# Layer 3's first sums and LayerNorms moved beside the last expert tiles of layer 2, in a four-layer conv/attention kernel

## The chip, the cores and the metric

The kernel runs on one core of a Trainium2 chip. Its time is that of the device, in microseconds; a kernel is timed several times and the median is given. Besides that, one execution is taken by the hardware profiler: from it come the busy times, waits and start times below. Times inside the profile count from the start of its span.

## The reference, cut to what matters

The input is four images of 256 channels by 32 x 32, so 4 x 1024 tokens of 256 numbers, float32. Layers 0 and 1 (a convolutional state-space block and a non-local block) come first and the change does not touch them. Layers 2 and 3 work on tokens:

```python
t = t + _L2_attn_ref(_ln_t(t), ...)     # softmax attention within an image
t = t + _L2_ffn_ref(_ln_t(t), ...)      # 8 experts, each token goes to its best 2
t = t + _L3_attn_ref(_ln_t(t), ...)     # "lambda" attention, see below
t = t + _L3_ffn_ref(_ln_t(t), ...)      # an LSTM over the 1024 tokens of each image
```

with, for the experts and for layer 3's attention,

```python
for e in range(E):
    h = gelu(xf @ W1[e] + b1[e])
    out = out + w_dense[:, e:e + 1] * (h @ W2[e] + b2[e])
...
sm = softmax(key, axis=1)                        # over the tokens of an image
lam = einsum('bnd,bne->bde', sm, value)          # 256 x 256 for each image
bn = (lam - mean) * rsqrt(var + BN_EPS)          # over images and columns
return einsum('bnd,bde->bne', query, bn * gamma + beta)
```

So each image's `lam` needs all its tokens after the experts, and the batch norm over `lam` needs all four images. The LSTM starts behind that and is a chain of 1024 steps.

## The kernel before, in words

**Experts (layer 2).** Each image's tokens are sorted by expert as soon as its attention and routing are done: POOL scatters them to a DRAM array `sorted`. The experts then run over tiles of 256 sorted places (`TS`), or 128 in a "half" tile. The 36 tiles (`NTILE`) are 17 "first" ones (`NFULL`), which hold only tokens known before the last image was routed; 16 "more" (`NMORE`); and 3 halves (`NHALF`). A half follows after every five or six of the "more" tiles. The last image's routing (`_head`, `_other_tiles`) runs as a generator in steps beside the first tiles. Up to three more halves stand behind a branch (`tc.If(need > NHALF)`), which this input does not take.

For each tile POOL fetches the expert's weights (2.2 MB, three buffers, two tiles ahead) and the rows by indirect DMA. PE transposes the rows (`pt`) and DVE copies them out (`uT`, L1279). PE makes 8 blocks of hidden units (`ph`, L1300), to which ACT applies the GELU (L1292), and two outputs (`po`, L1334), which DVE scales (`y`, L1339 and L1340). POOL scatters `y` to the DRAM array `results` (L1341), which has two places for each token, one for each of its two experts. In a half tile `ph` (L1314) has the tokens as its rows, DVE copies it out (`raw`, L1318) and PE transposes it back (L1322).

**Layer 3's attention** (`_layer3_attention`) starts behind the branch. For each image SP loads the two sums of four blocks (`y_in`, L1486, 0.5 MB each), DVE adds them to the tokens `s.xr` (L1491) and takes the statistics (L1495, L1496); a reciprocal root is made by 13 small DVE operations, ACT writes the normalised `rows` (L1476), and PE turns them to channels (`p_x`, L1442), from where DVE copies them to `u` (L1446). PE then makes the keys (`p_mm`, L1517), ACT moves them out (L1522), DVE takes the maximum (`top`, L1529), ACT the exponential (L1532). PE turns the keys back in eight pieces (`p_k`, L1542), which DVE copies (`kt`, L1544), and multiplies them with the rows (`p_u`, L1546); two more products give `lam` (L1556, L1560). PE also turns `s.xr` itself (L1442) and ACT copies it to a second array of channels (`x_l3`, L1445). The first image is put ahead by hand (`_in_order`, and `later` for what follows).

Behind the four images come the queries (L1573), the batch norm of `lam` (L1592), and the LSTM with its first products (`beside`, from L1674). The LSTM's constants (`_lstm_constants`: `fold`, `mask`, `shift`, `b_l`) and weights (`w_l`, `w_u`, `w_v`) are made and loaded right behind the branch. The LSTM's outputs are kept where `s.x` was.

**What sets the order.** Each engine works through its own queue in order. The tile framework's scheduler orders the instructions of a function by priorities and dependences, and inserts the waits; where the code says `_in_order`, the order as written stands. A tile pool that is opened where another was closed takes its memory, and its first users wait for the last ones of the old. Transfers on POOL's, SP's and ACT's queues share 16 DMA engines.

## Time and profile before

| what | us |
|---|---|
| median of 3 runs (3392.86 to 3399.31) | 3398.27 |
| the profiled execution | 3408.06 |
| its span | 3406.3 |
| PE, DVE, ACT, POOL busy | 3177.1, 1997.0, 1233.9, 378.8 |
| first tile's `ph` begins | 783.8 |
| one full tile, one half tile | 14.25, 8.3 |
| last expert matmul ends | 1306.7 |
| first product of layer 3 (`p_x`) | 1324.7 |
| `lam` of images 0, 1, 2, 3 (L1556) begins | 1363.8, 1394.1, 1418.5, 1442.2 |
| first LSTM step, first with a hidden state | 1472.1, 1475.3 |
| one LSTM step | 1.9 |

A profile line names the engine, the line of the code, the operation, and the tiles written and read, with a count. In a timeline the first number is the start and the second the length; a bracket at the end gives the idle time before it and what ended it. In a table by stretches, each pair is the busy time of an engine and its number of instructions; then come the clock granted to PE as a part of the full one, the share of the DMA engines and GB/s.

### The profile page before, as it was taken

Reading aid. Unit: us, or ns where it says so; the run is one execution under the profiler, and the core shown is the slowest. Engines: PE = TensorE matmul, PEld = TensorE weight load, DVE = VectorE, ACT = ScalarE, POOL = GpSimd, SP = SyncE. Lnnn points to the kernel's source line nnn. Section 1 sums busy time; section 2 is a strip of 40 time slices with the busy share of each in tenths; the row PEclk is TensorE's granted clock in tenths of the full one; section 3 lists DMA queues with packets and bytes.
Section 4 is the critical chain, followed back from the end, with each engine's and each line's share of the span. In section 5 each row is a group of like instructions: output and inputs, shape, how many; then the busy total and the mean of one; then the engine's idle time right before and its main releaser. Section 6 shows DMA issues by size and latency. Waiting matters only on the chain.

```text
span 3406.3 us, 146430 instructions
## 1 busy us (share of the span) xinstructions
PE 3177.1 (93%) x65186; PEld 2489.1 (73%) x65186; DVE 1997.0 (59%) x8389; ACT 1233.9 (36%) x5057; POOL 378.8 (11%) x468
## 2 busy tenths in 40 slices
PE   7788899998899996999999999999999999999888
PEld 4465344446788884688888888888888888888776
DVE  5696534452211115557777777776777767776666
ACT  4633222223222222433434334343343343443333
POOL 0083002223433330000000000000000000000000
PEclk9899899999999997999999999999999999999999
DMA  1291001115555654000000000000000000000000
GB/s 69 67 298 34 10 0 38 38 36 203 187 195 206 230 212 148 0 3 5 4 11 4 5 11 4 11 4 4 11 4 5 10 4 5 10 5 4 10 4 10
DMA packets 78058, 180.50 MB, mean 53 GB/s; under 512 B 6256, under 2 KB 63920, under 8 KB 72816
## 3 DMA queue, kind: packets, MB, share of 16 engines
q0 software_dynamic: 14880, 106.99, 8.5%
q1 hardware_dynamic: 60624, 59.12, 5.9%
q8 instruction: 511, 8.37, 1.0%
q10 hardware_dynamic: 1920, 5.00, 0.4%
q14 instruction: 123, 1.01, 0.1%
HBM read 111.26 MB, written 59.84 MB: 50 GB/s over the span
## 4 chain that ended last, share of the span: by engine, by line
PE 72%; DVE 14%; ACT 5%; issue 3%; DMA 2%; POOL 1%; ACTq 0%; DVEq 0%; POOLq 0%
PE p_c L1826 11%; PE p_c L1817 8%; PE ph L1300 6%; PE po L1334 6%; DVE turned L1867 6%; PE p_i L1817 5%; PE p_o L1826 5%; PE p_i L1826 5%; PE p_o L1817 5%; PE beside L1767 4%; PE p_mm L850 3%; PE p_s L814 2%; ACT a_o L1868 2%; DVE x L1880 2%; ACT th L1878 1%
## 5 line engine op out<-in xcount | busy, mean ns | idle before, releaser
L1868 ACT ACTIVATE add<-turned 128x8 f32<-128x8 f32 x1024 | 214.3, 209 | 1011.4 <-DVE turned L1867 1011.4
L1826 PE MATMUL p_c<-w_v,x 128*4 128x64 f32 x16368 | 416.7, 219 | 60.6 <-DVE x L1880 57.9
L1817 PE MATMUL p_c<-xg,shift 128*128 128x64 f32 x2048 | 446.0, 299 | 0.0
L1826 PE MATMUL p_o<-w_v,x 128*4 128x64 f32 x16368 | 417.8, 219 | 0.0
L1826 PE MATMUL p_i<-w_v,x 128*4 128x64 f32 x16368 | 417.4, 219 | 0.0
L1817 PE MATMUL p_i<-xg,shift 128*128 128x64 f32 x2048 | 407.7, 281 | 0.0
L1867 DVE STREAM_TRANSPOSE turned<-p_c 128x64 f32<-128x64 f32 x1024 | 255.7, 250 | 253.9 <-PE p_c L1826 220.0
L1817 PE MATMUL p_o<-xg,shift 128*128 128x64 f32 x2048 | 396.4, 275 | 0.0
L1817 PEld LDWEIGHTS p_c<-xg,shift 128*128 128x128 f32 x2048 | 304.9, 188 | 117.6 <-DVE turned L1867 0.4
L1826 PEld LDWEIGHTS p_c<-w_v,x 128*4 128x4 f32 x16368 | 227.9, 85 | 180.8 <-DVE x L1880 102.0
L1880 DVE TENSOR_TENSOR x<-a_o,th 128x8 f32<-128x8 f32 x1024 | 171.2, 167 | 246.0 <-ACT th L1878 246.0
L1817 PEld LDWEIGHTS p_o<-xg,shift 128*128 128x128 f32 x2048 | 311.4, 192 | 0.0
L1817 PEld LDWEIGHTS p_i<-xg,shift 128*128 128x128 f32 x2048 | 305.1, 188 | 0.0
L1826 PEld LDWEIGHTS p_o<-w_v,x 128*4 128x4 f32 x16368 | 281.9, 87 | 0.8 <-issue 0.5
L1826 PEld LDWEIGHTS p_i<-w_v,x 128*4 128x4 f32 x16368 | 281.6, 87 | 0.3
L1867 DVE STREAM_TRANSPOSE turned<-p_i 128x64 f32<-128x64 f32 x1024 | 271.9, 266 | 0.9 <-PE p_i L1826 0.7
L1292 ACT ACTIVATE hT<-ph,w 128x256 f32<-128x256 f32 (+1 forms) x288 | 131.3, 465 | 355.8 <-PE ph L1300 267.3
L1300 PE MATMUL ph<-uT,w 128*128 128x256 f32 x1056 | 241.6, 386 | 19.6 <-DVE uT L1279 11.3
L1867 DVE STREAM_TRANSPOSE turned<-p_o 128x64 f32<-128x64 f32 x1024 | 255.6, 250 | 0.9 <-PE p_o L1826 0.3
L1334 PE MATMUL po<-w,hT 128*128 128x256 f32 x1104 | 251.1, 380 | 2.7 <-ACT hT L1292 1.5
L1868 ACT ACTIVATE a_o<-turned 128x8 f32<-128x8 f32 x1024 | 213.3, 208 | 95.4 <-DVE cell L1871 4.5
L1300 PEld LDWEIGHTS ph<-uT,w 128*128 128x128 f32 x1056 | 203.2, 194 | 50.2 <-DVE uT L1279 12.1
(499 smaller groups left out, 4395.0 us busy)
## 6 DMA issues: line engine op xcount, KB each, us to landing
sorted<-zeros SPq DMA_DIRECT2D x32, 1032.0 KB
y_in<-results SPq DMA_DIRECT2D x16, 512.0 KB
x<-in_x_dram SPq DMA_DIRECT2D x8, 512.0 KB
tokens<-rows SPq DMA_DIRECT2D x4, 1024.0 KB
x<-tokens SPq DMA_DIRECT2D x8, 512.0 KB
out_dram<-x_l SPq DMA_DIRECT2D x64, 64.0 KB
results<-y,place POOLq DMA_INDIRECT x69
w_l<-in_w_l_dram ACTq DMA_DIRECT2D x1, 1092.0 KB
```

The source lines that it names most:

```text
L814: nc.tensor.matmul(p_s[:, h, :], q[:, k, q0 : q0 + P], u[:, k, b * L + h * W : b * L + (h + 1) * W], start=k == 0, stop=k == C - 1,)
L850: nc.tensor.matmul(p, v[:, n, bass.ts(c, P)], prT[:, n, :], start=n == 0, stop=n == TPI - 1,)
L1292: nc.scalar.activation(hT[:, n, : A * P], ph, AF.Gelu, bias=b1[:, n : n + 1])
L1300: nc.tensor.matmul(ph, w1[:, k, bass.ts(n, P)], uT[:, k, :], start=k == 0, stop=k == C - 1,)
L1334: nc.tensor.matmul(po, hT[:, n, bass.ts(a, P)], w2[:, n, :], start=n == 0, stop=n == NHC - 1,)
L1767: nc.tensor.matmul(p[bass.ts(i, R), :], rows[:, k, bass.ts(g, R)], w_u[:, k, at : at + GQ // GC], start=k == 0, stop=k == C - 1, tile_posi ...
L1817: nc.tensor.matmul(p[:, :H], shift[:, row * B : row * B + P], xg[n][:, g, bass.ts(i, H)], start=True, stop=t == 0,)
L1826: nc.tensor.matmul(p[R * i : R * i + B, :H], hs[:, t - 1, bass.ts(k, B)], w_v[:, k, i * GQ + g * H : i * GQ + (g + 1) * H], start=False, s ...
L1867: nc.vector.transpose(zt.rearrange("p c w -> p (c w)"), pz[g][:, :H])
L1868: nc.scalar.activation(dst.rearrange("p (c b) -> p c b", c=C), zt[:, :, :B], f)
L1878: nc.scalar.activation(th, cell[:, :, 1], AF.Tanh)
L1880: nc.vector.tensor_mul(h, a_o, th)
```

## The change

It does five things.

1. *The order of the tiles.* The "more" tiles are 14 that may hold tokens of any image, and then, interleaved with the three halves, two that hold only the last image's tokens or are empty. `NLAST` (31) is the number of tiles that may hold tokens of the first three images. `_other_tiles` places them by four kinds instead of two.
2. *Two sets of pools.* The experts are split into `_first_experts` (17 tiles) and `_last_experts` (the rest), with pools opened anew between them, since layer 3's buffers now share the memory with the second part. `hT` has one buffer and `uT` two.
3. *Image 0 and 1 beside the last tiles.* `_rows_to_u` holds the loads, sums, statistics, rows and transposes of an image as a generator. Those of image 0 run in steps beside tiles 32 and 33, those of image 1 beside tiles 34 and 35. The loads are declared independent of the scatters of tiles 31 to 35. They have two buffers of 0.5 MB. The instructions of these tiles stand in the order as written.
4. *Behind the branch:* keys of image 0 together with the rows of image 2, rows of image 3 with keys of image 1, then keys of images 2 and 3 with the transposes of x. The `p_k`/`p_u` loop issues the next transpose ahead of the last product. The keys have one buffer.
5. *x in place.* The channel copy of x is written over the tokens it came from (`s.x3`), and the LSTM's outputs get an array of their own. Weights of the LSTM and its constants are loaded or made after the attention.

```diff
+NLAST = (2 * (T - L) + E * (TS - 1)) // TS
...
+        m.order = [("first", i) for i in range(NFULL)]
+        m.order += [("more", i) for i in range(NLAST - NFULL)]
+        for i in range(NHALF):
+            m.order.append(("half", i))
+            if NLAST - NFULL + i < NMORE:
+                m.order.append(("more", NLAST - NFULL + i))
...
+            _layer2_attention(s, m)
+            _first_experts(s, m)
+        _last_experts(s, m)
...
+def _last_experts(s, m):
+    nc, tc = s.nc, s.tc
+    m.late, m.early = [], []
+    with ExitStack() as ctx:
+        wp = ctx.enter_context(tc.tile_pool(name="l3_w", bufs=1))
+        l3 = SimpleNamespace(
+            pool=ctx.enter_context(tc.tile_pool(name="l3", bufs=2)),
+            row=ctx.enter_context(tc.tile_pool(name="l3_row", bufs=2)),
+            y=ctx.enter_context(tc.tile_pool(name="l3_y", bufs=2)),
+            ps=ctx.enter_context(tc.tile_pool(name="l3_ps", bufs=2, space=PSUM)),
+            banks=0,
+            w=wp.tile([P, C, 2 * D], F32, name="w_kv"),
+        )
+        nc.scalar.dma_start(
+            l3.w, s.d["w_l3"][:, D : 3 * D].rearrange("(k p) n -> p k n", p=P)
+        )
...
+        parts = [_rows_to_u(s, l3, b) for b in range(2)]
...
+            fetched(NFULL + 1)
+            ahead = [_turned(s, m, NFULL)]
+            for j in range(NFULL, NTILE):
+                if j + 2 < NTILE:
+                    fetched(j + 2)
...
+                def beside(n):
+                    if j > NLAST:
+                        for _ in range(2 if m.order[j][0] == "half" else 1):
+                            next(parts[(j - NLAST - 1) // 2], None)
+                if j == NLAST:
+                    next(parts[0])
+                done = _worked(s, m, j, *ahead.pop(), lead, beside)
+                if j >= NLAST:
+                    _in_order(s, start)
...
+            for got in m.early:
+                for put in m.late:
+                    for one, other in ((got, put), (put, got)):
+                        tc.declare_no_dep(
+                            one.ins, other.ins, reason="these tiles hold the last image's tokens"
+                        )
...
+def _rows_to_u(s, l3, b, split=False):
...
+    def load():
+        g, k = todo[len(ys)]
+        at = k * T + (b * G + g) * W
+        y = l3.y.tile([P, TPB, D], F32, name="y_in")
+        got = nc.sync.dma_start(
+            y, s.results[at : at + W, :].rearrange("(j p) c -> p j c", p=P)
+        )
+        if b < B - 1:
+            l3.early.append(got)
+        ys.append(y)
...
+    load()
+    load()
+    yield
+    for i, (g, k) in enumerate(todo):
+        xr = s.xr[:, bass.ts(b * G + g, TPB), :]
+        nc.vector.tensor_add(xr, xr, ys[i])
+        if len(ys) < len(todo):
+            load()
+        yield
+        if k == 1:
+            for j in range(TPB):
+                stats = l3.pool.tile([P, nc.vector.BN_STATS_DIM], F32, name="stats")
+                nc.vector.bn_stats(stats, xr[:, j, :])
+                nc.vector.bn_aggr(mv[:, g * TPB + j, :], stats)
+                if j % 2:
+                    yield
...
+def _layer3_last_image(s, l3):
...
+        wq = wp.tile([P, C, D], F32, name="wq")
+        nc.scalar.dma_start(wq, s.d["w_l3"][:, 3 * D :].rearrange("(k p) n -> p k n", p=P))
...
+        order = (
+            (_keys(s, l3, 0, nc.vector), _rows_to_u(s, l3, 2)),
+            (_rows_to_u(s, l3, 3, split=True), _keys(s, l3, 1, nc.scalar)),
+            (_keys(s, l3, 2, nc.vector), chain(by_channel(0), by_channel(1))),
+            (_keys(s, l3, 3, nc.vector), chain(by_channel(2), by_channel(3))),
+        )
+        for parts in order:
+            for _ in _in_turn(*parts):
+                pass
+        for _ in queries():
+            pass
...
-        hs = s.x.rearrange("p c b l -> p (c b l)").rearrange("p (l s) -> p l s", s=S)
+        bias, fold, mask, shift = _lstm_constants(s, keep)
+        w_u = _weights(s, keep, "w_u")
+        w_v = _weights(s, keep, "w_v")
+        wq = keep.tile([P, C, D], F32, name="wq")
+        nc.scalar.dma_start(wq, s.d["w_l3"][:, :D].rearrange("(k p) n -> p k n", p=P))
+
+        hs = keep.tile([P, L, S], F32, name="hs")
```

Lines of the changed kernel that the prediction names: the adds are L1593, `shift` L1565, `rows` L1571, the transposes of the rows L1579, the y loads L1553, the first `ph` L1331.

## The prediction

> **What bounds the kernel now.** I read in this order: the page (who is busy), the chain that ended last, PE's timeline from the last expert tiles to the first LSTM step, and the other engines' timelines across the same stretch. The page says PE is busy 93% of the span and the chain that ended last lies 72% on PE, so what counts is where PE stands still and how long its stages last. PE around the branch:
>
> ```profile
> 1294.76 3.62 PE L1334 MATMUL po<-w,hT 128*128 128x256 f32 x16
> 1298.21 3.60 PE L1314 MATMUL ph<-w,uT 128*128 128x512 f32 x8
> ...
> 1303.08 3.62 PE L1334 MATMUL po<-w,hT 128*128 128x256 f32 x16
> 1324.72 2.16 PE L1442 MATMUL p_x<-ident,rows 128*128 128x128 f32 x8 [18.02 <-ACT rows L1476]
> 1328.64 3.63 PE L1517 MATMUL p_mm<-u_l,w_l 128*128 128x512 f32 x4 [1.76 <-DVE u_l L1446]
> ```
>
> Experts end at 1306.7 (call it E), and PE then stands 18.0 us. The other engines say what fills it: the last scatter, the load of its sums, two adds, LayerNorm.
>
> ```profile
> 1311.73 1.19 DVE L1411 TENSOR_REDUCE fold<-ident 128x32 f32<-128x128 f32 x4 [4.18 <-DMA w<-in_w_dram,half_rows]
> ...
> 1316.41 1.23 DVE L1491 TENSOR_TENSOR x<-x,y_in 128x1024 f32<-128x1024 f32 x1 [3.15 <-DMA y_in<-results]
> 1317.90 1.23 DVE L1491 TENSOR_TENSOR x<-x,y_in 128x1024 f32<-128x1024 f32 x1 [0.26 <-DMA y_in<-results]
> ```
>
> Both DVE and ACT go on 5.0 us after E (scatter issued by POOL at 1307.83, then 3.9 us to what waits for it); the first load, issued 1311.91, is added 4.5 us later. The stretches from E to the queries:
>
> ```profile
> 1306.70:1324.70 18.00, 0.00 (x1) 0.00 (x0) 9.72 (x34) 0.63 (x2) 0.97 (x1) 0.63 0.68 238
> 1324.70:1363.80 39.10, 30.57 (x97) 17.52 (x97) 29.66 (x86) 11.85 (x20) 0.00 (x0) 0.73 0.56 180
> 1363.80:1394.20 30.40, 26.64 (x117) 17.90 (x118) 23.11 (x79) 15.08 (x29) 0.00 (x0) 0.94 0.00 1
> 1394.20:1418.60 24.40, 23.49 (x113) 16.31 (x113) 12.22 (x24) 10.93 (x20) 0.00 (x0) 1.00 0.00 1
> 1418.60:1442.20 23.60, 20.59 (x87) 13.33 (x86) 7.35 (x16) 8.42 (x14) 0.00 (x0) 1.00 0.00 0
> ```
>
> Length, then busy time of PE, weight load, DVE, ACT, POOL, then granted clock. Image 0 costs 57 us from E to its p_mm L1556 (lam), the others 30, 24 and 24; the clock is 0.63 and 0.73 first and 1.00 at the end. Ahead of E there is almost no slack: the last five tiles (1253.3 to 1306.7, 53.4 us) keep PE busy 53.05 us. So work brought there is only hidden if PE never waits for it.
>
> **The change, part by part** (T = the end of tile 30; tiles are now 17 first, 14 more, half, more, half, more, half; 36 as before). The order on each engine is that of the built programs.
>
> *Start of the experts.* POOL issues rows of tiles 0 to 3 between the first and second weights, at 1.26 us an issue; DVE takes four place casts before uT of tile 0, where before it took two, the second waiting 5.74 us for rows that shared the queue with w1. Before, tile 0's ph started at 783.78. Four row pairs instead of one w (2.2 MB) ahead of it: -1.5 us, between -3 and +2.
>
> *Tile 16 to 17.* The pools are reopened: the first ph and gelu of tile 17 wait for the landing of tile 16's scatters, which the row above prices at 5.0 us after the last po. PE stands, and afterwards runs slow. A stop of that length is in the trace:
>
> ```profile
> 837.51 4.32 PE L1300 MATMUL ph<-uT,w 128*128 128x256 f32 x12 [5.26 <-DVE uT L1279]
> ```
>
> Twelve ph here take 4.32 us, at 7.07 us for 32 they take 2.65: 1.7 us more. [...] The weights of tiles 18 and 19 are issued only behind that landing (POOL waits); 5 MB with rows, and 2.5 MB took 6.3 us in the first tiles, so 12.6 us against the 14.25 us of tile 17: just covered; uncovered it would cost 0 to 4. Taken: 5.0 + 1.7 = +6.7, between +3 and +11. [...]
>
> *Tiles 31 to 35.* SP issues the y loads of image 0 when all scatters through tile 30 landed, T+5. y has two buffers, so each later load is issued after an add, and lands 4.5 us on. Adds (L1593, 1.22 us each) end at about T+11, 12, 17, 18, 22, 24, 28, 30. DVE is in order, and these adds stand ahead of y of tile 32, uT of tile 33 and raw of tile 33. Tile 31 takes 8.3 us, tile 32 14.25: PE wants uT at T+22.6, and gets it behind the sixth add and some BN_STATS at T+25 to 27 (2.4 to 4.2 us, taken 3.3, plus up to 1.7 of slow clock, taken 0.8). raw of tile 33 is wanted 1.7 us into the tile and comes after the eighth add: 3.0. Behind shift (L1565) ACT must write four rows (2.08 us) before PE's transposes, which stand ahead of the raw transposes: 1 us in tile 33, 2 in tile 35, and 1.5 for its second four rows, which ACT writes behind the gelus. The 32 transposes themselves, 0.13 us each: 4.2. Sum +15.8. Below: only the transposes count, +4.2 and one rows wait 2, +6. Above: every load 6.3 us instead of 4.5 because w of tiles 33 to 35 is on the way (+1.8 on three links in a row) and the clock drops twice: +24.
>
> *After the branch* (E' = its end now). PE's keys of image 0 wait for no landing. ACT stands at the wq issue until E'+5, then evicts; p_mm, 16 rows in 7.03 us at full clock (1396.35), end near E'+9. But DVE's first operation is the add of image 2's first load: 5.0 + 4.5, so E'+9.5. Then add, top, add, top at 1.22 us: E'+14.4; Exp 1.15: E'+16. The p_k/p_u loop takes 11.1 us (1431.07 to 1442.18), with the other adds among its copies about 13, and su: lam(0) at E'+31, against E+57. Image 1: shift of image 2 stands behind lam(0) on DVE, 8 rows at 0.51, 16 transposes, u copies: p_mm starts at E'+37.5, 7.0, top and Exp 4.2 (1403.2 to 1407.4), loop 12.5: lam(1) E'+63 against E+87.5. Images 2 and 3 at 24 to 25 each: lam(3) E'+112.5 against E+135.5. Gain 23.0. PE idles 5 us or more before the first Exp, so its first p_k/p_u pass is slow: 3.78 us against 1.99, 1.7 off.
>
> ```profile
> 1351.50 3.78 PE L1546 MATMUL p_u<-kt,rows 128*128 128x256 f32 x8 [0.30 <-DVE kt L1544]
> ...
> 1356.23 1.99 PE L1546 MATMUL p_u<-kt,rows 128*128 128x256 f32 x8
> ```
>
> Taken -21.3. Ends: -28 (image 1 follows image 0 at 28 us) and -14 (loads of images 2 and 3 each 2 us later, PE 3 us late through the branch itself, for which no row gives a price).
>
> x turned in place and the 64 x transposes keep their count and lie in PE's gaps as before; the cover is Exp and top (4.2 us an image), without it 8 us.
>
> *LSTM start.* Four b_l issues (1.97 us together), w_u, w_v, wq are now issued by ACT after the last lam, three b_l ahead of the first q; fold, mask, shift (1.19 + 0.28 + 0.19 and a memset) stand in the batch norm on DVE. The two overlap: +2. wq is wanted 6 us after its issue (lam_q, 1454.50) behind 1.5 MB of w_u and w_v: at 2.5 MB in 6.3 us plus landing it comes about 2 late. +4, between +1 and +8. Before, these loads had 140 us of cover.
>
> Extra small operations in the tables (about ten DVE, 0.16 us each) lie beside the first tiles, where DVE is busy 2.13 us of 14.2; uncovered 1.6. The w_kv issue on ACT between gelus of tiles 6 and 7 waits for the last image's scatters, which ended by 906 before, with tile 7's gelus later: 0, uncovered some us. The LSTM's own order is unchanged.
>
> Sum: -1.5 + 6.7 + 15.8 - 21.3 + 4 = **+3.7 us** on the profiled execution's 3408.06, which stands 9.8 over the median of 3398.27. On the median: 3402.
>
> **The rivals.** 0.2%, 6.8 us, is about what a measurement of this kernel tells from no change.
> *A, faster:* the loads land early enough that PE never waits in tiles 31 to 35, +6 instead of +15.8: -6.1, and with image 1 close behind image 0 (-26 instead of -21.3) -11: 3387 to 3392. For it: DVE is busy 8.37 us of those 53.4, and 30 us of added work would fit. Against: in DVE's order eight adds stand ahead of what PE needs. It decides where adds five and six end before tile 32's second po, T+22.
> *B, slower:* each link of the load chain is 1.8 us longer beside w and the clock drops twice, +24: 3410; with weights of tile 18 late, 3414. For it: the 310 GB/s in tiles at 820 to 831. Against: the first y load had two more loads of its kind and the 1 MB of w_l beside it and took 4.5 us.
> *C, the overlap does not come about:* keys of image 0 held by image 2's add to E'+20 or more, gain under 14: 3409 and up. Against: that add waits only for landing and load, 9.5 us.
>
> **How the numbers follow.** My case (net within 0.2%) 0.39; A 0.25; B 0.22; C 0.14. Half the terms are waits whose sizes I bounded, so the case's own range is 3394 to 3409, and A and B reach to 3384 and 3420. Faster 0.25, same 0.39, slower 0.36.
>
> **What would show it.** Right: PE idle about 5 us before tile 17 by a wait on a scatter; idle of 2 to 4 us before ph of tile 33 named DVE uT, with L1593 just before it on DVE; five last tiles of 66 to 72 us; first Exp 14 to 17 us after E'; lam(3) 108 to 117 us after E'. Wrong: if PE's last five tiles take under 62 us (A), or w of tile 18 is what PE waits for, or image 1's lam comes more than 70 us after E'.

## The result, and the profile after

| | median, us | lowest to highest | runs |
|---|---|---|---|
| kernel before | 3395.72 | 3392.23 to 3400.26 | 20 |
| changed kernel | 3403.30 | 3394.49 to 3421.93 | 20 |

The ratio of the two is 1.0028, with a 95% interval of 1.0017 to 1.0039: the change costs 6 to 13 us of some 3400. The changed kernel's runs spread over 27 us, those of the kernel before over 8. Of all runs below, one, of h2_one_early (5056.98 us at a mean clock of 0.549), is in a slower state of the chip and stands in no median or ratio here.

The profiled pair points the other way: 3396.70 us for the changed kernel (span 3394.7) against 3408.06 (span 3406.3). Its sum must close on the spans, and does, but it is not the sum of the medians: the execution of before that was profiled stands 12.3 us over the median of its 20 runs, that of the changed kernel 6.6 us under its own. PE's timeline of the changed kernel (start, length, engine, line, operation, and in brackets the idle time ahead with what ended it):

```profile
901.93 7.57 PE L1331 MATMUL ph<-uT,w 128*128 128x256 f32 x20 [10.29 <-ACT hT L1325]
...
1049.38 9.83 PE L1331 MATMUL ph<-uT,w 128*128 128x256 f32 x32 [3.81 <-DVE uT L1309]
...
1291.55 2.08 PE L1342 MATMUL ph<-w,uT 128*128 128x512 f32 x2 [15.04 <-DVE uT L1309]
...
1335.10 7.10 PE L1622 MATMUL bank<-u,w_kv 128*128 128x512 f32 x16 [1.24 <-DVEq L1511]
...
1346.89 0.55 PE L1647 MATMUL bank<-ident,key 128*128 128x128 f32 x3 [3.37 <-ACT key L1634]
1362.64 1.92 PE L1668 MATMUL bank<-w_kv,su 128*128 128x256 f32 x8
...
1433.91 2.00 PE L1668 MATMUL bank<-w_kv,su 128*128 128x256 f32 x8
```

Three stops stand out in the experts: 10.29 us at an early tile (the profiled execution of before stopped for 11.0 us in that stage too), 3.81 where the pools are reopened (and 9.83 us for 32 matmuls that take 7.07 at full clock), and 15.04 before tile 33. In return the 18 us of idle behind the branch are down to 1.24 and 3.37, and the last `lam` begins at 1433.9 instead of 1442.2, although the experts end 26.7 us later (1333.4). The stretches from the end of tile 30 to the last `lam` (length, then busy time of PE, weight load, DVE, ACT, POOL, granted clock, DMA share, GB/s):

```profile
1254.00:1276.50 22.50, 22.50 (x103) 17.96 (x101) 4.57 (x9) 5.96 (x16) 6.79 (x7) 1.00 0.75 276
1276.50:1291.55 15.05, 0.01 (x2) 0.01 (x1) 12.96 (x37) 0.00 (x0) 0.99 (x1) 0.62 0.57 178
1291.55:1333.40 41.85, 39.29 (x164) 27.56 (x165) 19.01 (x60) 16.16 (x40) 5.74 (x5) 0.93 0.23 81
1333.40:1362.60 29.20, 22.49 (x99) 16.38 (x98) 18.55 (x49) 9.13 (x14) 0.97 (x1) 0.88 0.47 143
1362.60:1390.00 27.40, 24.43 (x120) 16.89 (x119) 16.24 (x63) 19.06 (x39) 0.00 (x0) 1.00 0.05 17
1390.00:1413.50 23.50, 21.38 (x97) 14.72 (x95) 10.39 (x20) 6.94 (x12) 0.00 (x0) 1.00 0.00 1
1413.50:1433.90 20.40, 17.49 (x71) 11.51 (x69) 7.34 (x15) 6.51 (x10) 0.00 (x0) 1.00 0.00 0
```

The second row is the cost: for 15 us PE does nothing, DVE works 12.96 of them, and the clock falls to 0.62. What DVE does there, and what it had waited for:

```profile
1275.63 1.23 DVE L1593 TENSOR_TENSOR x<-x,y_in 128x1024 f32<-128x1024 f32 x1 [12.30 <-DMA y_in<-results]
1277.10 1.23 DVE L1593 TENSOR_TENSOR x<-x,y_in 128x1024 f32<-128x1024 f32 x1 [0.25 <-DMA y_in<-results]
...
1288.61 1.22 DVE L1593 TENSOR_TENSOR x<-x,y_in 128x1024 f32<-128x1024 f32 x1
...
1291.07 0.42 DVE L1309 COPY uT<-bank 128x256 f32<-128x256 f32 x1
1292.90 1.19 DVE L1593 TENSOR_TENSOR x<-x,y_in 128x1024 f32<-128x1024 f32 x1
```

The first add comes 21.6 us after the end of tile 30, and `uT` of tile 33 stands behind six adds. SP could issue the first load only at 1266.46, 12.5 us after that end, because the scatter of tile 30 stood in POOL's queue behind the weights of tile 33: those landed at 1265.5, the scatter at 1265.9. First SP's queue, then POOL's:

```profile
1266.46 23.75 SPq L1553 DMA_DIRECT2D y_in<-results  x8
...
1255.38 0.97 POOL L1276 DMA_INDIRECT w<-in_w_dram,half_rows  x1 [2.58 <-issue]
1256.65 0.99 POOL L1371 DMA_INDIRECT results<-y,place  x1 [0.30 <-DVE raw L1345]
```

The transfers issued from 1253 to 1300 (operation, size, median us from issue to landing) have the scatters at 8.8 us; what waited for the last scatter in the kernel before went on 3.9 us after its issue:

```profile
y_in<-results SPq DMA_DIRECT2D x8, 512.0 KB, 4.3
results<-y,place POOLq DMA_INDIRECT x4, 8.8
w<-in_w_dram,half_rows POOLq DMA_INDIRECT x2, 9.8
```

The whole profile sorts its 69 scatters by this: the 38 that were issued with no expert weights on their way landed after 2.4 us (median; 2.4 to 4.7), the 31 others after 8.8 (5.0 to 11.5). The loads add to it. The first two `y_in`, issued while the weights of tile 34 were on their way, landed after 9.2 and 10.1 us, the six later ones after 3.8 to 4.8.

The whole ledger of the profiled pair, after minus before, in us:

| stage | difference | how it is read |
|---|---|---|
| up to the end of attention, same order | -4.2 | its last `x` at 769.7 against 773.9 |
| start of the experts | -2.3 | first `ph` 777.3 against 783.8, less the line above |
| stop before `uT` at 830 | -0.7 | 4.56 against 5.26 |
| stops at 880 to 912 | -0.7 | 10.29 against five stops of 11.0 together |
| pools reopened (tile 16 to 17) | +6.6 | 3.81 idle, 9.83 - 7.07 |
| tiles 17 to 30 | +2.1 | what the experts' difference of 33.2 (556.1 - 522.9) leaves; two `uT` waits of 0.63 and 1.25 are seen |
| tiles 31 to 35 | +25.9 | 79.3 against 53.4 |
| end of experts to the last `lam` | -35.0 | 100.5 against 135.5 |
| last `lam` to the first LSTM step | 0.0 | 29.9 in both; before had 3.4 us of half clock there, after none |
| LSTM | -3.4 | before had 6.8 us of half clock in its first steps, after none |
| sum | -11.7 | spans: 3394.7 - 3406.3 = -11.6 |

### The profile page after: what moved, and what is told of

Its sections match the earlier page's. It is cut to its first block, busy times and chain, and to the rows that moved or that the text cites. A ratio compares the mean times of both kernels' runs of the same rounds, so it can differ in the third digit from the quotient of the medians.

```text
span 3394.7 us, 146693 instructions
## 1 busy us (share of the span) xinstructions
PE 3163.7 (93%) x65186; PEld 2483.7 (73%) x65186; DVE 2000.2 (59%) x8394; ACT 1236.8 (36%) x5065; POOL 380.0 (11%) x468
## 4 chain that ended last, share of the span: by engine, by line
PE 46%; DVE 8%; ACT 4%; issue 1%; DMA 1%; ACTq 0%; SPq 0%; DVEq 0%; POOLq 0%
PE p_c L2012 11%; PE p_c L2003 8%; DVE turned L2053 6%; PE p_i L2003 5%; PE p_o L2012 5%; PE p_i L2012 5%; PE p_o L2003 5%; PE beside L1953 4%; ACT a_o L2054 2%; DVE hs L2066 2%; ACT th L2064 1%; PE beside L1860 1%; PE p_u L1656 1%; PE beside L1893 0%; PE bank L1622 0%
## 5 line engine op out<-in xcount | busy, mean ns | idle before, releaser
L2012 PE MATMUL p_c<-w_v,hs 128*4 128x64 f32 x16368 | 416.0, 219 | 60.8 <-DVE hs L2066 57.9
L2012 PE MATMUL p_o<-w_v,hs 128*4 128x64 f32 x16368 | 416.7, 219 | 0.0
L2012 PE MATMUL p_i<-w_v,hs 128*4 128x64 f32 x16368 | 416.5, 219 | 0.0
L2012 PEld LDWEIGHTS p_c<-w_v,hs 128*4 128x4 f32 x16368 | 227.4, 86 | 182.2 <-DVE hs L2066 102.3
L2066 DVE TENSOR_TENSOR hs<-a_o,th 128x8 f32<-128x8 f32 x1024 | 172.0, 168 | 245.9 <-ACT th L2064 245.9
L2012 PEld LDWEIGHTS p_o<-w_v,hs 128*4 128x4 f32 x16368 | 281.2, 87 | 0.5 <-issue 0.5
L2012 PEld LDWEIGHTS p_i<-w_v,hs 128*4 128x4 f32 x16368 | 281.1, 87 | 0.2
L1331 PE MATMUL ph<-uT,w 128*128 128x256 f32 x1056 | 245.5, 391 | 24.5 <-DVE uT L1309 14.1
L1331 PEld LDWEIGHTS ph<-uT,w 128*128 128x128 f32 x1056 | 206.1, 197 | 56.5 <-DVE uT L1309 16.7
```

What stands on the lines that cost most here:

```text
L1331: nc.tensor.matmul(ph, w1[:, k, bass.ts(n, P)], uT[:, k, :], start=k == 0, stop=k == C - 1)
L2012: nc.tensor.matmul(p[R * i : R * i + B, :H], hs[:, t - 1, bass.ts(k, B)], w_v[:, k, i * GQ + g * H : i * GQ + (g + 1) * H], start=False, s ...
L2066: nc.vector.tensor_mul(h, a_o, th)
```

## The experiments

All were timed against the kernel before on the same chip; its medians there were 3397.83 (runs e1 to e4), 3398.52 (f1, g1, f3), 3397.16 (h1, h2) and 3398.43 (j1 to j3). Beside the time I give for each run the **half-clock time**: twice the share that the granted clock is short of 1, times the span. It comes in steps of 7 us from rounding. In the kernel before it lies between 163 and 184 us in every run; in the changed kernel it lies between 156 and 191 in sixteen of twenty, and at 212 to 233 in the four slowest (3414 to 3422). Over the twenty runs of the changed kernel, time rises by 0.37 us for each us of half-clock time; over the 81 runs of the kernel before that were timed beside the experiments, by 0.33. A **spell** is an unbroken stretch at half clock; a profile shows its length, and of a run without a profile I call it long where the half-clock time stands over 200 us.

**Do the row waits ahead of the rows spread the runs?** In tiles 18 to 30 the scheduler set the cast of `place`, three tiles ahead, in front of `uT` on DVE.

```diff
-                if j >= NLAST:
-                    _in_order(s, start)
+                _in_order(s, start)
```

> The changed kernel with tiles 17 to 30 in the order as written too, so that DVE takes place of the next tile at its own place and no longer place of a tile three ahead before uT of the next one. Theory 1 (the spread of the changed kernel, 3394 to 3422, and about 7 us of its median are PE waits for uT behind that place, which waits for rows still on their way): in tiles 18 to 30 no PE wait named uT, 14.25 us each, median near 3396, spread under 10 us. Rival (the loss is elsewhere): median 3400 to 3406 and the same spread.

Measured: 3402.98 us (3395.62 to 3420.82, 12 runs), ratio 1.0023 (1.0008 to 1.0038). The two `uT` waits in tiles 18 to 30 went and tile 31 began 2.5 us sooner, but three of twelve runs still lay above 3415. So the small waits are real and worth about 2 us, and they are not the spread, as the rival had it.

**Is the stop at 902 the issue of `w_kv`?** ACT has that issue between two GELUs, behind the last image's scatters:

```profile
900.93 0.37 ACTq L1447 DMA_DIRECT2D w_kv<-in_w_l_dram  x1
901.41 1.20 ACT L1325 ACTIVATE hT<-ph,w 128x256 f32<-128x256 f32 x3 [19.12 <-DMA results<-y,place]
```

```diff
-        nc.scalar.dma_start(
+        nc.sync.dma_start(
             l3.w, s.d["w_l3"][:, D : 3 * D].rearrange("(k p) n -> p k n", p=P)
```

> The changed kernel with the w_kv load issued by SP in place of ACT. Theory 2 (ACT stands at that issue until the last image's scatters have landed, and PE with it: 10.3 us idle and 2.9 us of slow clock in one first tile): the idle goes, 8 to 13 us less up to the end of the first tiles. Rival (the scatters hold that stretch anyway, as in the kernel before, where one tile takes 29.3 us without this load): the idle is split over several waits, under 3 us less.

Measured: 3404.61 us (3400.53 to 3411.22, 11 runs), ratio 1.0020 (1.0011 to 1.0029): no gain. With the issue on SP, PE stops almost as long, one tile on, and for rows. PE's timeline of this run:

```profile
903.70 3.72 PE L1363 MATMUL po<-w,hT 128*128 128x256 f32 x16 [1.57 <-DVE y L1369]
...
917.40 7.86 PE L1331 MATMUL ph<-uT,w 128*128 128x256 f32 x28 [9.97 <-DVE uT L1309]
```

So ACT's wait was only the last link. The rows that `uT` waits for here landed right behind a weight load, in POOL's queue, where the last image's sorted scatters stand ahead of both; that these scatters set the stretch is the likely reading, and no run tests it. None of the eleven runs has a long spell, although nothing was changed at the LSTM's start.

**Does a later start of the two images avoid the stop before tile 33?** The sums of images 0 and 1 begin one tile later, beside tiles 33 to 35, with three steps at each place in half tiles instead of two.

```diff
-        parts = [_rows_to_u(s, l3, b) for b in range(2)]
+        parts = chain(*(_rows_to_u(s, l3, b) for b in range(2)))
...
-                    if j > NLAST:
-                        for _ in range(2 if m.order[j][0] == "half" else 1):
-                            next(parts[(j - NLAST - 1) // 2], None)
+                    if j > NLAST + 1:
+                        for _ in range(3 if m.order[j][0] == "half" else 1):
+                            next(parts, None)
```

> The changed kernel with the sums and LayerNorms of images 0 and 1 begun one tile later, beside tiles 33 to 35, with three steps in place of two in a half tile. Theory 3 (PE's 15.0 us before tile 33 are DVE standing at the first add for a load that comes late): uT of tile 33 comes in time, tiles 31 to 35 take 62 to 68 us in place of 79.3, time 8 to 15 us less. Rival (DVE's own 27 us of sums and statistics do not fit beside three tiles): the wait moves to uT of tile 34 and raw of tiles 33 and 35, under 4 us less.

Measured: 3417.51 us (3405.40 to 3419.14, 6 runs), ratio 1.0045 (1.0030 to 1.0061). The one stop of 15 us became several, and tiles 31 to 35 took 81 us all the same. PE's timeline:

```profile
1282.97 0.66 PE L1350 MATMUL ph<-ident,raw 128*128 128x128 f32 x4 [2.44 <-DVE raw L1345]
1292.27 3.78 PE L1331 MATMUL ph<-uT,w 128*128 128x256 f32 x8 [6.91 <-DVE uT L1309]
...
1326.05 1.95 PE L1579 MATMUL bank<-ident,rows 128*128 128x128 f32 x4 [4.83 <-ACT rows L1571]
```

So it is not the place of the first add alone: the work of two images is too much for these tiles. Four of the six runs had a long spell of half clock besides; the profiled one is read below.

**No image beside the tiles in the source.** The steps are put behind tile 35; what the scheduler then draws forward is its own choice.

```diff
-                    if j > NLAST:
+                    if False:
...
-                if j == NLAST:
-                    next(parts[0])
```

> The changed kernel without the overlap: images 0 and 1 are summed and normalised behind tile 35, all else as changed. Theory 4 (the stage before the branch pays 25 us for what saves less): tiles 31 to 35 take 53 to 56 us; lam of image 3 begins 112 to 122 us after the last expert matmul in place of 100.6; 4 to 14 us less than the changed kernel. Rival (the overlap is worth its price and the loss lies in the first tiles): 5 us more than the changed kernel or worse.

Measured: 3411.09 us (3390.95 to 3413.02, 7 runs), ratio 1.0040 (1.0027 to 1.0053). The scheduler still set adds among the tiles (stops of 8.68 and 4.01 us), tiles 31 to 35 took 71.0 us, and the last `lam` came at 1423.8, 10 us ahead of the changed kernel. The two runs without a long spell ended at 3390.95 and 3399.76, the other five, at 211 to 225 us of half clock, at 3409 to 3413. An order that is 10 us better up to the last `lam` was hidden by the clock. It does not say what no overlap costs, since the scheduler made one.

**What starts a spell.** The profiled run of e3_later has the longest of the profiles so far. Its stretches, the first ending where the spell begins, the second the spell, the third as long again:

```profile
1458.49:1461.90 3.41, 3.41 (x27) 3.28 (x26) 0.39 (x3) 0.66 (x4) 0.00 (x0) 1.00 0.00 0
1461.90:1506.30 44.40, 44.04 (x704) 38.85 (x707) 16.87 (x86) 11.15 (x52) 0.00 (x0) 0.50 0.01 2
1506.30:1550.70 44.40, 44.40 (x1486) 37.63 (x1479) 31.68 (x154) 17.45 (x95) 0.00 (x0) 1.00 0.02 5
```

PE is busy without a gap in the stretch before the spell (by the profile's account, which models when a matmul ends), hardly pauses in the spell, and does half as many matmuls in it (704 against 1486). No idle window stands ahead of it. What stands in the stretch before is this, on PE:

```profile
1459.41 1.93 PE L1903 MATMUL var<-avg,sq 128*128 128x1 f32 x16
1461.20 1.34 PE L1828 MATMUL beside<-lam,wq 128*128 128x256 f32 x4
```

Sixteen matmuls that load 128 columns of weights and stream one. The first test makes them stream 128 and reads one column of the result:

```diff
+            WV = P if n == 0 else 1
...
-                        var[:, i : i + 1], sq[:, k, bass.ts(i, P)], s.avg[:, :1],
+                        var[:, i, :], sq[:, k, bass.ts(i, P)], s.avg[:, :WV],
```

> The changed kernel, with the 16 variance matmuls ahead of the LSTM (first input gates only) made 128 columns wide instead of 1; only column 0 is read. It costs about 0.7 us of TensorE (a group of four 128-column matmuls took 0.69 us in the profile, sixteen one-column ones 1.93). Theory: the half-clock spells at the start of the LSTM begin in a 3.41 us window that is filled with one-column matmuls and so counts as idle; then the long spells go, the half-clock time of every run lies below 185 us, nothing ends above 3408 us, and the median falls from 3403.3 to 3397-3400. Rival: the spells come from elsewhere (the LSTM's own small steps); then the spread stays, a run in four or five ends above 3412 us, and the median stays at 3402-3405.

Measured: 3402.32 us (3398.07 to 3411.53, 12 runs), ratio 1.0012 (1.0003 to 1.0020). The half-clock time lies between 163 and 191 us; none of the runs has a long spell. The median fell by 1 us only, so the numbers that I set for the theory were missed on that side and by two runs at 3411: the slow fifth went, the middle did not. Twelve runs without a long spell prove little by themselves, since e2_wkv_sp had eleven.

The opposite test does them twice over, which changes no result:

```diff
-            for i in range(TT):
+            for i in (*range(TT), *range(TT)) if n == 0 else range(TT):
```

> The changed kernel with the one-column variance matmuls ahead of the LSTM made twice over (1.9 us more, same result). Theory: windows with few streamed columns put the clock to half, whatever TensorE's busy share; then nearly every run has a half-clock window there, spells of over 211 us of half-clock time come in half of the runs or more rather than in 4 of 20, and the median rises to 3408-3416. Rival: one-column matmuls count as work; then the median is 1.5 to 2 us above the changed kernel's (3405) and long spells are as rare as there.

Measured: 3419.96 us (3407.97 to 3427.04, 6 runs), ratio 1.0057 (1.0038 to 1.0077). Four of six runs have 205 us of half clock or more (three of them over 211, as the theory had it), the median lies above the theory's 3408 to 3416, and 1.9 us more of such matmuls cost some 10 us (by the two ratios) to 17 (by the two medians). PE's timeline and the stretches of the profiled run:

```profile
1454.62 3.71 PE L1903 MATMUL var<-avg,sq 128*128 128x1 f32 x32
```

```profile
1459.20:1510.40 51.20, 50.84 (x855) 45.00 (x857) 19.19 (x97) 12.49 (x60) 0.00 (x0) 0.50 0.01 2
1510.40:1561.60 51.20, 51.11 (x1710) 42.99 (x1695) 36.68 (x178) 20.04 (x109) 0.00 (x0) 1.00 0.02 5
```

The spell is 51.2 us: fifteen windows of 3.41 us, the grid on which the clock changes in every profile of this study. In before 21 of the 22 half-clock stretches, and in after 17 of 18, last 3.41 to 20.48 us and a whole multiple of 3.413; the last one, 7.88 and 7.52 us, is cut off by the program's end.

The other profiles show what stands ahead of a spell. Eleven of them (before, after and nine runs) have the sixteen one-column matmuls ahead of the LSTM. In nine the whole group fell into one window, with 1300 to 1556 columns streamed there and PE busy throughout, and in all nine the next window was at half clock. In g1_before_late most of the group fell into one (1302 columns), and the next was at half clock too. In after it was split between two windows of 1810 and 2318 columns, and the clock stayed full. In f1_wide the group, now 128 columns wide, again fell whole into one window, of 3332 columns, and the clock stayed full as well. The group in after, the group in f1_wide and the window behind that one:

```profile
1456.53 1.93 PE L1903 MATMUL var<-avg,sq 128*128 128x1 f32 x16
1464.66 2.03 PE L1904 MATMUL var<-avg,sq 128*128 128x128 f32 x16
1467.17:1470.59 3.42, 3.42 (x24) 3.17 (x22) 1.87 (x12) 0.90 (x5) 0.00 (x0) 1.00 0.00 0
```

So in these profiles a busy TensorE went to half clock behind the windows with the whole group or most of it, of 1300 to 1556 columns, and not behind those of 1810, 2318 and 3332. How long it stayed there went with the place of the group in its window. Where it began 1.2 to 1.4 us into the window (before, e1, e4, f3, h1, j2), the half-clock window behind it streamed 1540 columns, and the clock came back after it. Where it began 0.6 to 1.0 us in (h2, e3, e2), that window streamed 1031 to 1286, and the spell lasted 34.1, 44.4 and 17.1 us; in g1, 1.9 us in, it streamed 1286, and the spell lasted 23.9.

**What keeps it at half.** For all profiles of this study (before, after and the twelve runs) I cut the span from about 35 to 1510 us into the 3.413 us windows in which the clock changes, and counted the columns that the matmuls stream in each (a matmul counts where it starts). Matmuls whose weights have 32 columns or fewer count a quarter, because the kernel sets those of the LSTM four side by side (at full clock sixteen of them with 64 columns each took 0.41 us in after, and eight with 128 columns and weights of 128 took 1.04 us in before, 1024 columns both times); that weighting is my estimate.

```
columns streamed    windows at full clock        windows at half clock
in the window       all     next one at half     all     next one at full
under 1200          262     239                  248       0
1200 to 1300         26      13                   23       0
1300 to 1400         13      11                   10       2
1400 to 1500         24       8                   37       9
1500 to 1600         36       7                   97      15
1600 to 2000         92       3                   55      47
2000 and more      4881       0                  252     208
```

Two things limit the upper rows. Of the 239 windows under 1200 that led to half clock, PE was busy for less than 0.9 of the window in 238, so these rows are about idle time as much as about columns. And of the 23 under 1200 that stayed at full clock, 21 hold matmuls of an earlier layer norm (L209 of the changed kernel) with weights of 8 columns that run one behind another: there I take the quarter to be wrong, and unweighted they streamed 2560 to 4096 (one of 512 columns took 0.59 us in after). Outside that layer norm the full-clock windows with PE busy for 0.9 or more part cleanly: the eleven with 1047 to 1556 columns, those of the variance matmuls, were all followed by half clock, and none with 1809 or more was.

This LSTM streams 2300 to 2560 in most windows at full clock, and of the full-clock windows with 2000 or more none led to half. At half clock its step takes 3.23 us instead of 1.87, and it streams 1280 to 1440; of the 47 half-clock windows between 1300 and 1500 eleven led back. Where a spell came at its start, it lasted from 3.4 us (before) to 51.2 (j3_twice). My estimate from the table was that a spare matmul of 128 columns in each of its first eight steps would lift it out:

```diff
+        spare = ps.tile([P, P], F32, name="var")
...
+            if t < 8:
+                nc.tensor.matmul(spare, s.ident, s.avg, start=True, stop=True)
```

> The changed kernel with the spare 128x128 matmul in each of the LSTM's first eight steps and nothing else. In the profiles, an LSTM that runs at half clock streams 1280 to 1440 weighted columns in a window of 3.41 us, and windows of 1472 or 1540 are followed by full clock. Theory: 128 columns more in each step (a step is 3.23 us at half clock) lift the window to some 1540, so a spell ends in two or three windows: half-clock time below 192 us, no run above 3411, median 3400-3403. Rival: the clock does not go by the streamed columns; then spells of 40 us come as before (4 of 20 runs above 211 us of half clock), with 1.4 us more in all: median 3403-3407.

Measured: 3406.31 us (3396.57 to 3412.79, 8 runs), ratio 1.0024 (1.0013 to 1.0035). The half-clock time is 156 to 191 us, as expected, with no long spell; the profiled run has a spell of 10.2 us at the first step. The median is the rival's, though, and two runs ended above the 3411 that I had set: the spare matmuls stand on the path (a step takes 2.07 us with one, 1.87 without: 1.6 us in eight). Nor did they do what they were for: a step at half clock grew with them to between 3.5 and 3.8 us, and the three windows of that spell streamed 1408, 1376 and 1504 columns, not 1540. That they shorten spells is not shown by eight runs; that they cost time is.

**Do the late loads matter?** The changed kernel issues the LSTM's weights and constants when the LSTM opens. The kernel before with that part alone:

```diff
-    w_u = _weights(s, s.wpool, "w_u")
-    w_v = _weights(s, s.wpool, "w_v")
...
+        bias, fold, mask, shift = _lstm_constants(s, keep)
+        w_u = _weights(s, keep, "w_u")
+        w_v = _weights(s, keep, "w_v")
+        wq = keep.tile([P, C, D], F32, name="wq")
+        nc.scalar.dma_start(wq, s.d["w_l3"][:, :D].rearrange("(k p) n -> p k n", p=P))
```

> The kernel before, with the LSTM's weights, query weights and constants loaded and made when the LSTM's pool opens, as the changed kernel does; nothing else is moved. Theory: the late loads and the wait on them (1.23 us on wq in the changed kernel) are what brings the half-clock spells; then some runs end above 3408 us and the median rises by 4-7 us to 3402-3405. Rival: the late loads cost their wait alone; then the median is 3398-3401, and no run ends above 3406 us.

Measured: 3410.67 us (3401.70 to 3415.11, 9 runs), ratio 1.0032 (1.0022 to 1.0043): 12 us slower, more than expected. From the first `beside` to the first hidden step it takes 38.4 us, against 27.1 before. Waits of 1.04, 0.87 and 2.71 us stand there, the last on `wq`, and the clock after them:

```profile
1447.87 2.05 PE L1643 MATMUL beside<-lam,wq 128*128 128x256 f32 x4 [2.71 <-DMA wq<-in_w_l_dram]
```

```profile
1448.00:1453.00 5.00, 5.00 (x16) 4.37 (x17) 0.66 (x2) 0.85 (x3) 0.00 (x0) 0.50 0.00 0
...
1463.00:1468.00 5.00, 5.00 (x17) 4.37 (x16) 1.15 (x7) 0.87 (x4) 0.00 (x0) 0.50 0.01 3
```

Six of nine runs have 198 us of half clock or more, which none of the 81 runs of the kernel before has. So in the kernel before the late loads and constants bring long spells. The other way round, the changed kernel with these weights loaded behind the first `lam`, into the buffer that the last tiles' weights leave:

```diff
-        w_u = _weights(s, keep, "w_u")
-        w_v = _weights(s, keep, "w_v")
-        wq = keep.tile([P, C, D], F32, name="wq")
-        nc.scalar.dma_start(wq, s.d["w_l3"][:, :D].rearrange("(k p) n -> p k n", p=P))
+        w_u, w_v, wq = s.lstm_w
...
+            if i == 0:
+                held = m.w.tile([P, NEXP], F32, name="w")
+                s.lstm_w, at = [], 0
+                for n, x in (
+                    (NW["w_u"], s.d["w_u"]), (NW["w_v"], s.d["w_v"]), (D, s.d["w_l3"][:, :D])
+                ):
+                    w = held[:, at : at + C * n].rearrange("p (k n) -> p k n", k=C)
+                    got = nc.gpsimd.dma_start(w, x.rearrange("(k p) n -> p k n", p=P))
+                    tc.add_manual_dep(
+                        got.ins, l3.done.ins.name,
...
+                        reason="behind the first lam",
+                    )
+                    s.lstm_w.append(w)
+                    at += C * n
```

> The changed kernel, with the LSTM's two weight tensors and its query weights loaded behind the first lam into the buffer that the last expert tiles' weights leave, instead of when the LSTM's pool opens; the constants stay late. Theory: in the kernel before, the late loads alone cost 12 us (3410.67 against 3398.52) and brought the spells of half clock; in the changed kernel they do the same in a part of the runs. Then no run ends above 3409 us, the half-clock time lies below 190 us, and the median falls from 3403.3 to 3395-3400. Rival: in the changed kernel the LSTM starts cold for another reason (the batch norm's gaps, the constants); then the spread stays, runs end above 3412 us, and the median is 3401-3405.

Measured: 3401.18 us (3393.63 to 3405.82, 11 runs), ratio 1.0012 (1.0003 to 1.0020). No long spell; the half-clock time is 163 to 184 us, the same as before's. The four runs in twenty of the changed kernel that lie at 3414 to 3422 have no counterpart here, but e2_wkv_sp kept the late loads and had none in eleven either: that the loads make the tail in the changed kernel fits and is not shown. The median is 4.0 us over the kernel before: the rival's value, and what the rest of the change costs at an equal clock.

**One image instead of two.** Image 0 alone goes beside the last five tiles, at half the rate; image 1 beside the keys of image 0, and so on.

```diff
-        parts = [_rows_to_u(s, l3, b) for b in range(2)]
+        parts = _rows_to_u(s, l3, 0)
...
-                    if j > NLAST:
-                        for _ in range(2 if m.order[j][0] == "half" else 1):
-                            next(parts[(j - NLAST - 1) // 2], None)
+                    if j > NLAST and (n % 2 or m.order[j][0] == "half"):
+                        next(parts, None)
...
-            (_keys(s, l3, 0, nc.vector), _rows_to_u(s, l3, 2)),
-            (_rows_to_u(s, l3, 3, split=True), _keys(s, l3, 1, nc.scalar)),
-            (_keys(s, l3, 2, nc.vector), chain(by_channel(0), by_channel(1))),
-            (_keys(s, l3, 3, nc.vector), chain(by_channel(2), by_channel(3))),
+            (_keys(s, l3, 0, nc.scalar), _rows_to_u(s, l3, 1)),
+            (_keys(s, l3, 1, nc.scalar), _rows_to_u(s, l3, 2)),
+            (_rows_to_u(s, l3, 3, split=True), _keys(s, l3, 2, nc.scalar), by_channel(0)),
+            (_keys(s, l3, 3, nc.vector), chain(*(by_channel(b) for b in range(1, B)))),
```

> The changed kernel, with image 0 alone beside the last five tiles, at half the rate of steps, and images 1, 2 and 3 each one stage later behind the branch (image 1 beside the keys of image 0). Theory: with two images DVE is the bound in those tiles (busy 12.96 us of the 15.05 before tile 33), and the half that is left fits; then the five tiles end at 1313-1322 us instead of 1333.4, the first lam comes 29-33 us later, the last at 1418-1426 instead of 1433.9, and the median is 3393-3398. Rival: the wait of the first add for its rows (12.3 us) sets the stop, not DVE's work; then the tiles still end after 1325, the last lam comes at 1432 or later, and the median is 3402-3408.

Measured: 3389.60 us (3386.03 to 3392.83, 6 runs), ratio 0.9971 (0.9959 to 0.9983): 9 us faster than the kernel before, and by the medians 14 faster than the changed one. The stretches from tile 31 to the last `lam`:

```profile
1252.00:1276.36 24.36, 24.36 (x112) 19.55 (x110) 3.70 (x8) 5.98 (x16) 7.47 (x8) 1.00 0.71 259
1276.36:1283.98 7.62, 0.00 (x0) 0.00 (x0) 6.84 (x16) 0.00 (x0) 1.31 (x1) 0.69 0.45 141
1283.98:1320.10 36.12, 35.65 (x150) 26.19 (x150) 14.62 (x43) 11.62 (x32) 5.93 (x6) 0.92 0.22 81
1320.10:1346.70 26.60, 21.57 (x92) 14.73 (x92) 17.30 (x51) 11.25 (x21) 0.97 (x1) 0.94 0.50 160
1346.70:1371.40 24.70, 22.32 (x110) 15.60 (x108) 22.02 (x84) 18.39 (x39) 0.00 (x0) 1.00 0.32 101
1371.40:1396.20 24.80, 23.04 (x115) 16.30 (x114) 9.21 (x16) 14.83 (x31) 0.00 (x0) 1.00 0.00 1
1396.20:1421.90 25.70, 23.05 (x82) 15.49 (x83) 9.27 (x18) 6.51 (x10) 0.00 (x0) 0.87 0.00 0
```

The stop before tile 33 is half as long (7.62 us against 15.04), and the experts end at 1320.1 instead of 1333.4. From there to the last `lam` it is 101.8 us, against 100.5 with two images: the second image bought nothing behind the branch, since its rows fit beside the keys of the first. The stop that is left is the rival's. DVE's timeline:

```profile
1276.62 1.23 DVE L1592 TENSOR_TENSOR x<-x,y_in 128x1024 f32<-128x1024 f32 x1 [13.45 <-DMA y_in<-results]
...
1282.31 1.22 DVE L1592 TENSOR_TENSOR x<-x,y_in 128x1024 f32<-128x1024 f32 x1
1283.51 0.42 DVE L1309 COPY uT<-bank 128x256 f32<-128x256 f32 x1
```

The first add still waits 13.45 us for its rows, with `uT` behind it in DVE's queue.

**One image, with early loads.** The edits of f3_one and h1_early together.

> Image 0 alone beside the last five expert tiles, as in the run before (3389.6, half-clock time 156-183 us), with the LSTM's weights loaded behind the first lam as well. Theory: the wait on the query weights and the cold start of the LSTM go; median 3384-3388, no run above 3392. Rival: the loads were hidden there, since those runs already had little half-clock time; median 3388-3391, or more where the 1.8 MB delay the rows of images 1 to 3.

Measured: 3395.75 us (3383.63 to 3404.43, 11 runs), ratio 1.0000 (0.9989 to 1.0010). The theory fell, and so did the rival's 3388 to 3391. The wait on `wq` was gone and the rows were in time (the last `lam` not later against the experts' end), but five of the eleven runs had 190 to 204 us of half clock and more than 3399 us, and the profiled one a spell of 34.1 us from 1448.3, right behind the one-column matmuls:

```profile
1445.45 1.93 PE L1916 MATMUL var<-avg,sq 128*128 128x1 f32 x16
1447.23 1.11 PE L1841 MATMUL beside<-lam,w 128*128 128x256 f32 x4
```

So a wait ahead of the LSTM is not needed for a spell, and removing it is no cure. In the profile of h1_early, with the same loads, the group filled a window too, but 1.2 us into it, and the clock came back after one window; here it began 0.6 us in. The group's place in its window differs between the profiles (0.6 to 1.9 us in), so chance may have a part in it. Why eleven runs of h1_early had no long spell and this one several stays open, since the other runs have no profile.

**One image, with the start of the LSTM kept warm.** The edits of f3_one, f1_wide and j2_fill.

> Image 0 alone beside the last five expert tiles (3389.6 us when it ran alone), with the variance matmuls ahead of the LSTM 128 columns wide, and with one spare 128x128 matmul in each of the LSTM's first eight steps; the spare results are read by nobody. Theory: the two together keep the 3.41 us windows at the LSTM's start above some 1500 streamed columns, so no spell of half clock lasts over 10 us there; half-clock time below 185 us in every run, none above 3394, median 3386-3390. Rival: eight spare matmuls lie on the LSTM's path (0.17 us each, with 0.7 us for the wide ones: +2) and the spells come all the same: median 3391-3396.

Measured: 3387.85 us (3386.14 to 3390.62, 6 runs), ratio 0.9969 (0.9957 to 0.9981): the fastest kernel here, 10.6 us under the kernel before, with the smallest spread. The half-clock time is 149 to 163 us, and the profiled run has no half-clock window in its LSTM:

```profile
1454.90:1506.10 51.20, 51.13 (x1631) 43.39 (x1630) 35.05 (x171) 19.40 (x106) 0.00 (x0) 1.00 0.02 4
```

Whether it beats f3_one (3389.60) six runs of each can't tell.

## Why the prediction was right, and where it was not

The total was 3402 us; the median is 3403.3. The net is less close: +3.7 was forecast on a median of three runs of before, 3398.27, and measured is +7.6 between the two medians of twenty, +4.0 in h1_early, which has no long spells. And the total is right in part by luck. Two of its terms were off by 10 us and more in opposite directions (+10.1 and -13.7), and one cause, the clock at the start of the LSTM, was not in it. Of the five signs that I had set for being right, only the wait on a scatter ahead of tile 17 came about as said (3.8 us, for 5); the stop before tile 33, the five tiles, the first exponential (12.2 us after E', for 14 to 17) and the last `lam` all lay outside their numbers. None of the three signs for being wrong came either.

- *Start of the experts*, -1.5: measured -2.3.
- *Tile 16 to 17*, 5.0 + 1.7 = +6.7: measured 3.81 + 2.76 = +6.6. The stop was shorter and the slow clock with it longer: 6.83 us of half clock from 1048.0, against 3.41 from 837.1 around the row at 837.51. The scatter that it waits for was issued with no weights ahead and landed after 2.4 us. The weights of tile 18 were not awaited.
- *`w_kv` on ACT*, costed at 0 because the scatters "ended by 906 before". The cover was not there: PE stops 10.29 us. Against the profiled execution of before it costs nothing, since that one stopped 11.0 us in the same stretch. But the profile of g1_before_late, whose experts are those of before, stops there for 1.63 and 3.43 us, 5.1 together. So the step is worth between -0.7 and +5.2, and I had read one execution's stops as the kernel's. The experts of that profile take 514.6 us, those of the profiled execution of before 522.9: a good part of the 12.3 us by which the latter stands over its median may lie here, which two profiles can't decide. e2_wkv_sp shows that the queue of the issue is not what matters.
- *Tiles 17 to 30*, nothing predicted: about +2, from `uT` behind a cast that waits for rows (e1_order removes it).
- *Tiles 31 to 35*, +15.8 (bounds 6 and 24): measured +25.9, beyond the upper bound. The mechanism was named (adds ahead of `uT` of tile 33 on DVE) and the size was wrong at its first term, "SP issues the y loads when all scatters through tile 30 landed, T+5". It was T+12.5, and the first load then took 9.2 us, not 4.5. I priced the landing by the scatter behind the last tile, with no expert weights in the queue ahead of it (5.0 us after the tile, 3.9 after its issue); here the scatter was issued at T+2.7, right behind a 2.2 MB weight load, and the scatters of that stretch took 8.8 us to land. The first add came at T+21.6 instead of about T+10, and six adds ran while PE waited or was about to. The stop was 15.0 us, not 3.3 + 3.0 = 6.3. The other 10.9 us (transposes, slow clock, and 2.56 us of small gaps in the third stretch) stand against 9.5 that I had for these.
- *After the branch*, -23.0 + 1.7 = -21.3 (bounds -28 and -14): measured -35.0. The first `lam` came at E'+29.2 (predicted E'+31), the second at +56.6 (+63), the last at +100.5 (+112.5). I gave image 1 32 us and the two others 24 to 25 each, from before's stages; they took 27.4, 23.5 and 20.4. That the transposes of x and the rows, now spread over the stages, are the reason is likely and not tested.
- *LSTM start*, +4: the profile shows 0.0, the runs show more. In the kernel before the same late loads cost 12 us (g1_before_late); in the changed kernel, undoing them for the weights brings the ratio from 1.0028 (1.0017 to 1.0039) to 1.0012 (1.0003 to 1.0020) without a run of 3414 to 3422 (h1_early), which the runs of e2_wkv_sp, with the late loads, don't have either. The waits are about as small as I had them; the price in the kernel before is the clock behind them, which I counted at the other stops and not here.

Rival A (faster, PE never waiting in the five tiles) fell with the adds: five and six ended at T+33.9 and T+35.9, the condition was T+22. Rival B (slower by longer links and the clock) had the size of what happened in the tiles (+24, measured +25.9), not its course: only the first two loads were late, the later links were as short as I had them, and the clock fell once, for 17.1 us, where I had it fall twice at the price of the row at 837.51; no run shows a price for a second fall. The larger gain behind the branch gave it back. Rival C (the overlap not coming about) fell: the keys began 1.7 us after E'.

Idle time was not the only thing that stood ahead of a half clock: the 17.1 us of it from 1280.1 began 3.6 us into the stop before tile 33, but the 3.41 us ahead of the spell in e3_later were busy for 3.41.

## What to carry to other kernels

Price the landing of a transfer by a row that shares its queue with the same neighbours: the scatter behind the last tile was waited for 3.9 us after its issue, those behind a weight load took 8.8 to land, and every add, copy and tile behind it paid. When work is moved into the shadow of other work, move as much as the in-order engine between them can carry (here one image's adds on DVE, not two): the second half brought 1 us behind the branch and cost 13 ahead of it. And where two orders differ by a few us, look at the spread and the clock of the runs before the median: a better order (e4_behind, 3391 at best) can be hidden by a worse clock.

## What the runs showed of the hardware that was not expected

TensorE went to half clock behind a window of 3.41 us in which it was busy for 3.41 (e3_later). Sixteen one-column matmuls (1.93 us) that fell into one 3.41 us window with 1300 to 1556 columns in all were followed by half clock in nine profiles of nine; split between two windows, in one profile, or made 128 columns wide, in two, they were not. In the 14 profiles, of 4881 full-clock windows with 2000 columns or more, none was followed by half clock. This LSTM ran at either clock, at 2300 to 2560 columns in most windows at full clock and 1280 to 1440 at half, and over all 14 profiles none of the 271 half-clock windows under 1300 columns and 11 of the 47 between 1300 and 1500 led back to full. Over the changed kernel's runs, one us of half clock went with 0.37 us of time.

In the profile of the changed kernel a scatter issued on POOL's queue while a load of 2.2 MB was on its way there took 8.8 us to land (median of 31), one without took 2.4 (median of 38).
